# Reordering the first group of four batches: routers, one block sum and the first loads

## The chip, the cores and the metric

The kernel runs on one core of one Trainium2 chip. The metric is the device time of one execution in microseconds (us). Five engines work side by side, each on its own queue of instructions: PE (matrix products, its weight loads shown as PEld), DVE (vector), ACT (scalar), POOL (general) and SP, which here only issues loads and stores. The order of instructions on each engine is written out by hand in the program; semaphores make an engine wait for the data or the buffer that another one gives it.

## The reference

Four layers follow each other, each added to its input. x has 8 batches of 256 tokens with 1024 features, all in float32. Layer 0, where the change lies, is cut here to its core:

```
base   = x @ W.T
logits = x @ Wr.T + 5 * one_hot(language)          # 8 experts
gates  = softmax over the best 2 logits, 0 elsewhere
h      = x @ A[e].T for all 8 experts              # rank 16 each: 128 rows
x      = x + base + 2 * sum_e (h[e] * gates[e]) @ B[e].T
...
x = x + x @ (W1 + coeff * (2*mask - 1)) + b1       # layer 1, a mask for each batch
x = x + x @ W2[adapter].T                          # layer 2, a matrix for each batch
x = x + 2 * (x @ B3[adapter].T) @ A3[adapter].T    # layer 3, rank 16
```

The products are split: every float32 matrix is taken as a rounded part (hi) and a rest (lo), and hi x hi, lo x hi and hi x lo are summed.

## The kernel before

The batches are worked in two groups (g = 0, 1) of four, each group as two pairs of batches; `pair_of(g, 0)` is the first pair worked (p0, pair 1 in group 0) and `pair_of(g, 1)` the second (p1, pair 0). Features lie in 8 slices k of 128.

Layer 0 takes its 2x2 block product of W and the two pairs in Winograd's form: seven block products instead of eight, with sums S1 to S4 of the blocks A11 to A22 of W and sums T1 to T4 of the blocks B11 to B22 of x. `L0_PRODUCTS` lists them; each fills two slots s (halves h), and two more slots (4 and 5) hold only products of x with the experts' matrix A. So group 0 has slots 0 to 15: 0, 1 A11 x B11; 2, 3 A12 x B21; 4, 5 the second pair's expert products; 6, 7 S1 x T1; 8, 9 S4 x B22; 10, 11 S2 x T2; 12, 13 S3 x T3; 14, 15 A22 x T4. Blocks that go into a slot are numbered in order (`items`); block i is split on ACT into `whi` (hi, `highs`) and on DVE into `wlo` (lo, `lows`), with five and four buffers; so a split of hi stands five blocks ahead of the buffer's last use, a split of lo four.

`l0_slot(n)` writes one slot: first what leaves the accumulators (`l0_evacuate`: the copies U1 at slot 2 and C11 at slot 6 on ACT; V at 8, W at 10 and so on as sums on DVE), then the splits, then the slot's further works (`l0_works`, a table by slot made with `at(s, ...)`; negative keys are run ahead of the splits), then the matmuls (`l0_main`, with works in the middle of a product from the table `l0_mids`). The accumulators are tiles of a pool with two buffers; `chain` takes a new two at slots 0, 6 and 10, so slot 6 takes over the two of slots 0 to 5. `head` is slots 0 and 1 written by hand in quarters of a block, so that the first matmuls start on small loads.

The works of group 0 that matter here:

- `logits(p)`: 16 records of small matmuls into a bank, copied to `lg` by ACT. `by_token(p)` turns it over on PE (`pt`). `router(p)` is some 21 small DVE instructions, with one ACT instruction (`ex`, the exponential) two thirds of the way, and ends in the gates; `expand(p)` repeats them to 128 columns (`gx`). `gates_by_rank(p)` turns those over on PE (`pg`) and copies to `gt`. `gate(p)` multiplies `gt` with the experts' products `ph` on DVE and splits the result into `ghi` (ACT) and `glo` (DVE), which the last matmuls of slot 5 (p0) and those of slot 9 (p1) use with `lb`, the experts' B.
- `la_parts`: splits A into `laghi`, `laglo`.
- `less` (T1, T3): negates a block of x in place on ACT, and adds another block by a load that accumulates, issued by POOL. `s1_add`, `s3_add`: POOL adds the identity to a block, then such a load. `s4_add`: a copy on ACT and such a load; before the change group 0 instead adds two blocks on DVE for S4.
- `constants`: 8 small DVE instructions on the language, coefficient and adapter numbers.

SP issues the first loads one after the other in the order at the end of the kernel; each waits for the load issued eight before it.

Of the kernel before, what the change touches and what calls it, by code (L numbers as in the profile page):

```python
# [34 lines left out]
def kernel(ctx: ExitStack, tc: tile.TileContext, x, lang, coeff, ids,  # L35
# [73 lines left out]
    lbs = [cst.tile([P, K * P], FR, name=f"lb{n}") for n in range(2)]  # L109

    def load_constants():
        nc.sync.dma_start(wrs, wr)
        nc.sync.dma_start(lang_i, lang.rearrange("(a b) -> a b", a=1).to_broadcast([P, NB]))
        nc.sync.dma_start(c_sb, coeff.rearrange("(a b) -> a b", a=1).to_broadcast([P, NB]))
        nc.sync.dma_start(ids_raw, ids.rearrange("(a b) -> a b", a=1))
        nc.sync.dma_start(b1_sb, b1)
# [59 lines left out]
    def pair_of(g, j):  # L176
        return 2 * g + 1 - j
# [124 lines left out]
    def logits(p):  # L302


        g, j = p // 2, 1 - p % 2
        pl = bank(j, f"pl{p}")
        for k in range(K):
            c = 32 * (k % 4)
            mm(pl[c:c + 32, :], wrs[:, k, :], X[g][:, j, k, :], start=(k < 4), stop=(k >= 4))  # L309
        lgs[p] = gp.tile([P, N], F32, tag="lg", name=f"lg{p}", bufs=3)  # L310
        copy(lgs[p], pl)

    def by_token(p):
        pts[p] = bank(1 - p % 2, f"pt{p}")
# [80 lines left out]

    def gate(p):
        tt(gts[p], phs.pop(p), gts[p], ALU.mult)
        split_gates(p, gts[p])

    def gate_difference(g):  # L400

# [259 lines left out]
    def l0_works(g):  # L661


        p0, p1 = pair_of(g, 0), pair_of(g, 1)
        w = {}

        def at(s, *fs):
            w.setdefault(s, []).extend(fs)

        def add(name, h, src):  # L670
            nc.gpsimd.dma_start(quad(g, name)[h], src, accum_op=ALU.add)

        def s1_add(h):
            fold_quad(quad(g, "S1")[h], h)
            add("S1", h, w0[1, 2 + h])

        def s3_add(h):
            t = quad(g, "S3")[h]
            copy(flat(t), flat(quad(g, "S2")[h]))
            fold_quad(t, h)  # L680
            add("S3", h, w0[1, 2 + h])

        def s4_add(h):
            copy(flat(quad(g, "S4")[h]), flat(quad(g, "S2")[h]))
            add("S4", h, w0[0, 2 + h])

        def less(h, name, j, i):

            t = flat(quad(g, name)[h])
            nc.scalar.mul(t, t, -1.0)  # L690
            add(name, h, x[pair_of(g, j)][:, 4 * i + 2 * h:4 * i + 2 * h + 2])

        def both(f, *args):
            return [lambda h=h: f(h, *args) for h in range(2)]

        def subs(o, a, b):
            return [lambda h=h: sub(g, o, a, b, h) for h in range(2)]

        def lb_parts():
            copy(lbs[0], lb_raw)  # L700
            tt(lbs[1], lb_raw, f32(lbs[0]), ALU.subtract)

        if g == 0:
            at(1, *both(less, "T1", 1, 0), constants)
            at(2, *both(s1_add))
            at(3, lambda: router([p0]), lambda: expand(p0))
            at(4, lb_parts)
            at(-5, lambda: gate(p0))
            at(5, *subs("S2", "A11", "S1"))
            at(6, lambda: [tt(flat(quad(0, "S4")[h]), flat(quad(0, "S4")[h]),  # L710
                              flat(quad(0, "S2")[h]), ALU.add) for h in range(2)])
            at(6, lambda: router([p1]), lambda: expand(p1))
        else:
            at(0, *both(s1_add), *both(less, "T1", 1, 0))
            at(2, lambda: expand(p0))
            at(3, *subs("S2", "A11", "S1"))
            at(4, *both(s4_add))
            at(-5, lambda: gate(p0))
            at(5, lambda: expand(p1))
        at(4, *both(less, "T3", 1, 1))  # L720
        at(7, *subs("T2", "T1", "B22"))
        at(7, *both(s3_add))
        at(8, lambda: gate(p1), lambda: gate_difference(g))
        for h in range(2):
# [24 lines left out]
    def l0_mids(g):  # L749


        p0, p1 = pair_of(g, 0), pair_of(g, 1)
        if g == 0:
            return {2: lambda: by_token(p0), 3: lambda: logits(p1),
                    4: lambda: [by_token(p1), gates_by_rank(p0)],
                    7: lambda: gates_by_rank(p1)}
        mids = {0: lambda: proj_pair(1, 0), 1: lambda: rank_pair(1, 1, (0, 1)),
                2: lambda: gates_by_rank(p0), 6: lambda: gates_by_rank(p1)}
        mids.update({s: lambda: fill(2) for s in (3, 4, 5)})
        mids[-5] = lambda: fill(2)  # L760
        return mids
# [28 lines left out]
    def l0_slot(n):  # L790
        _, g, s, _ = slots[n]
        f = first[n]
        store()
        if s >= 7:
            load_unit(64 * g + s - 7)
        w = works[g]
        if s == 0 and g:
            G[g] = region(GC[g], f"c{g}", [P, 4, 4, N], F32)
        evacuate()
        l0_evacuate(g, s)  # L800
        if (g, s) == (0, 0):
# [11 lines left out]
        if g == 0 and s == 1:  # L813
            la_parts(0, 4, 8)
        if g or s > 1:
            l0_main(g, s)
        for u in merges.get(n + 1, []):
            merge_scale(u)

    def head():  # L820

        chain(0, 0)
        for s in range(2):
            for k in range(2):
                c = slice(k * 512, (k + 1) * 512)
                for i in (2 * s, 2 * s + 1):
# [6 lines left out]
                la_parts(0, 2 * s + k, 2 * s + k + 1)  # L833
                product(s, 0, [k], start=(s == 0))
                experts(0, pair_of(0, 0), 2 * s, 2 * s + k, k)
            folded.update((2 * s, 2 * s + 1))
        logits(pair_of(0, 0))


    pos_tile = {}  # L840
# [1 line left out]
    def main(n):  # L842
# [15 lines left out]
        if kind == "L1":  # L858
            if u == 0:
                hls["L2", q] = hl_tile(GX[q // 2], f"hl2_{q}")  # L860
        else:
            if u == 0:
                i = 2 - 2 * (q % 2)
                xt2 = G[q // 2][:, i:i + 2].rearrange(
                    "p j a (b t) -> p j (a b) t", b=2)
                xts[q, 2] = xt2
                xts[2 * q], xts[2 * q + 1] = xt2[:, 0], xt2[:, 1]
            if q % 2:
                if u == 1:
                    mid = [lambda: proj_pair(q - 1, 2)]  # L870
                if u == 3:
                    mid = [lambda: rank_pair(q - 1, 3, (2, 3))]
                if 5 <= u < 9:
                    mid = [lambda: fill(2)]
            if q == 1:
                if u == 13:
                    mid = [lambda: [logits(p) for p in (2, 3)]]
# [122 lines left out]
    for h in range(2):  # L1000
        for k in range(2):
            m = 2 * h + k
            load_x(0, 0, m, m + 1)
            nc.sync.dma_start(W0[0, "A11", h][:, k], w0[0, h][:, k])
            if m != 1:
                k0, k1 = ((0, 2), None, (2, 4), (4, 8))[m]
                nc.sync.dma_start(LA[0][:, k0:k1], la[:, k0:k1])
    load_x(0, 0, 4, 6)
    load_w0(0, "A12", 0)
    load_constants()  # L1010
    load_x(0, 0, 6, 8)
    load_w0(0, "A12", 1)
    for h in range(2):
        load_w0(0, "A21", h)
    load_x(0, 1, 0, 4)
# [95 lines left out]
```

## Time and profile before

| what | us or share |
|---|---|
| median of 3 runs (lowest to highest) | 623.31 (623.06 to 623.85) |
| profiled execution | 622.18 |
| its span, first to last instruction | 620.2 |
| PE busy | 598.4 (96%) |
| DVE busy | 477.2 (77%) |
| ACT busy | 383.6 (62%) |
| POOL busy | 129.8 (21%) |
| mean granted PE clock | 0.989 |
| PE busy in the first 81.34 us of the span | 67.17 |

The last row is group 0 up to slot 9. A sum of durations from the profile is compared with the profiled execution's own time, 622.18 us, of which 620.2 is the span; the median of the runs is 1.13 us above it. In the listings below a group or timeline line gives engine, line of the program, instruction, the tile written and the tiles read.

### The profile page before, as it was taken

Reading aid. Unit: us, or ns where it says so; the run is one execution under the profiler, and the core shown is the slowest. Engines: PE = TensorE matmul, PEld = TensorE weight load, DVE = VectorE, ACT = ScalarE, POOL = GpSimd, SP = SyncE. Lnnn points to the kernel's source line nnn. Section 1 sums busy time; section 2 is a strip of 40 time slices with the busy share of each in tenths; the row PEclk is TensorE's granted clock in tenths of the full one; section 3 lists DMA queues with packets and bytes.
Section 4 is the critical chain, followed back from the end, with each engine's and each line's share of the span. In section 5 each row is a group of like instructions: output and inputs, shape, how many; then the busy total and the mean of one; then the engine's idle time right before and its main releaser. Section 6 shows DMA issues by size and latency. Waiting matters only on the chain.

```text
span 620.2 us, 8932 instructions
## 1 busy us (share of the span) xinstructions
PE 598.4 (96%) x3244; PEld 502.0 (81%) x3244; DVE 477.2 (77%) x557; ACT 383.6 (62%) x453; POOL 129.8 (21%) x172
## 2 busy tenths in 40 slices
PE   8699699999999999999999999999999999999995
PEld 7477488888888888888778778888888888888884
DVE  5348967889879999777664786788987999967852
ACT  4527456668667898653545655656866798864331
POOL 0211314001321212221310132611431111321000
PEclk9899899999999999999999999999999999999998
DMA  8964379447586677589952498945758667756504
GB/s 271 379 139 69 75 182 238 148 168 278 202 272 236 226 282 273 170 337 316 293 134 41 117 239 189 257 153 185 288 171 283 224 243 266 274 166 218 191 1 135
DMA packets 39101, 129.17 MB, mean 208 GB/s; under 512 B 4754, under 2 KB 6162, under 8 KB 38290
## 3 DMA queue, kind: packets, MB, share of 16 engines
q1 hardware_dynamic: 34594, 112.62, 51.5%
q0 software_dynamic: 4320, 15.73, 13.9%
q8 instruction: 25, 0.41, 0.3%
q10 hardware_dynamic: 144, 0.26, 0.1%
q14 instruction: 18, 0.15, 0.1%
HBM read 120.21 MB, written 8.39 MB: 207 GB/s over the span
## 4 chain that ended last, share of the span: by engine, by line
PE 89%; DVE 5%; ACT 3%; issue 2%; DMA 1%; ACTq 0%; DVEq 0%
PE po L523 38%; PE mm L591 25%; PE po L532 20%; DVE wlo L68 2%; PE pl L309 1%; PE pf L462 1%; PE pb L434 1%; DVE x L68 1%; ACT whi L289 1%; ACT x L690 1%; DVE A L68 1%; PE ph L617 1%; DVE c L68 1%; PE ph L619 1%; PE ph L618 1%
## 5 line engine op out<-in xcount | busy, mean ns | idle before, releaser
L523 PE MATMUL po<-hl,whi 128*128 128x512 f32 x1016 | 254.5, 392 | 0.0
L523 PEld LDWEIGHTS po<-hl,whi 128*128 128x128 f32 x1016 | 182.8, 189 | 32.7
L68 DVE TENSOR_TENSOR wlo<-raw,whi 128x1024 fp32r<-128x1024 f32 x128 | 160.9, 1267 | 1.3 <-issue 1.2
L532 PEld LDWEIGHTS po<-hl,wlo 128*128 128x128 f32 x1016 | 137.6, 190 | 11.3 <-issue 2.5
L289 ACT CAST whi<-raw 128x1024 fp32r<-128x1024 f32 x128 | 133.7, 1048 | 17.9 <-PE mm L591 8.4
L532 PE MATMUL po<-hl,wlo 128*128 128x256 f32 x1016 | 142.3, 283 | 0.0
L591 PE MATMUL mm<-whi,whi 128*128 128x512 f32 x224 | 89.4, 399 | 4.1 <-DVE c L68 3.3
L591 PE MATMUL mm<-wlo,whi 128*128 128x512 f32 x224 | 88.6, 395 | 0.0
L236 POOL TENSOR_TENSOR raw<-raw,ident 128x128 f32<-128x128 f32 x72 | 57.5, 801 | 117.6 <-DMA raw<-in_w 100.0
L258 ACT ACTIVATE raw<-raw,negc,c 128x1024 f32<-128x1024 int32 x64 | 79.5, 1242 | 3.4 <-DMA raw<-in_mask 3.4
L591 PE MATMUL mm<-whi,wlo 128*128 128x512 f32 x224 | 71.3, 394 | 0.0
L68 DVE TENSOR_TENSOR raw<-raw,w 128x1024 f32<-128x1024 f32 x56 | 70.2, 1254 | 0.7 <-POOL w L236 0.7
L68 DVE TENSOR_TENSOR wlo<-x,whi 128x1024 fp32r<-128x1024 f32 (+1 forms) x38 | 45.0, 1193 | 32.0 <-ACT whi L289 10.5
L236 POOL TENSOR_TENSOR w<-w,ident 128x128 f32<-128x128 f32 x28 | 27.6, 985 | 168.5 <-DMA w<-in_w 122.4
L591 PEld LDWEIGHTS mm<-whi,whi 128*128 128x128 f32 x224 | 42.7, 191 | 15.5 <-issue 4.9
L591 PEld LDWEIGHTS mm<-whi,wlo 128*128 128x128 f32 x224 | 42.5, 190 | 9.7 <-DVE wlo L68 0.4
L591 PEld LDWEIGHTS mm<-wlo,whi 128*128 128x128 f32 x224 | 42.8, 191 | 8.9
L564 ACT COPY c<-po 128x512 f32<-128x512 f32 (+1 forms) x34 | 18.8, 552 | 47.0 <-PE po L532 47.0
L289 ACT CAST whi<-A 128x1024 fp32r<-128x1024 f32 x26 | 27.3, 1048 | 33.1 <-PE mm L591 15.5
L289 ACT CAST whi<-x 128x1024 fp32r<-128x1024 f32 x34 | 35.3, 1049 | 14.7 <-PE mm L591 14.7
L567 ACT ACTIVATE sum<-po,b_sb 128x512 f32<-128x512 f32 (+1 forms) x36 | 23.1, 641 | 30.7 <-PE po L532 30.7
L68 DVE TENSOR_TENSOR c<-mm,c 128x1024 f32<-128x1024 f32 x20 | 24.2, 1219 | 19.9 <-PE mm L591 19.9
(126 smaller groups left out, 534.4 us busy)
## 6 DMA issues: line engine op xcount, KB each, us to landing
raw<-in_mask SPq DMA_DIRECT2D x64, 512.0 KB, 5.0
raw<-in_w SPq DMA_DIRECT2D x64, 512.0 KB, 4.8
w<-in_w SPq DMA_DIRECT2D x28, 512.0 KB, 3.7
out<-c SPq DMA_DIRECT2D x31, 256.0 KB, 3.2
A<-in_w SPq DMA_DIRECT2D x14, 512.0 KB, 8.5
x<-in_x SPq DMA_DIRECT2D x6, 1024.0 KB, 8.4
x<-in_x POOLq DMA_DIRECT2D x12, 512.0 KB, 7.8
A<-in_w POOLq DMA_DIRECT2D x10, 512.0 KB, 7.3
```

The lines of the kernel that those rows point to most:

```text
L68: nc.vector.tensor_tensor(o, a, b, op)
L236: (eng or nc.gpsimd).tensor_tensor(t, t, ident, ALU.add)
L258: nc.scalar.activation(f32(raws[n]), raws[n], AF.Identity, bias=negc[:, b:b + 1], scale=c2[:, b:b + 1])
L289: copy(prep_hi(i), flat(source(i)))
L309: mm(pl[c:c + 32, :], wrs[:, k, :], X[g][:, j, k, :], start=(k < 4), stop=(k >= 4))
L434: mm(pb[c:c + 32, j * T:(j + 1) * T], l3b[b][:, k, :], xts[b][:, k, :], start=(k < 4), stop=(k >= 4))
L462: mm(po[:, i * T:(i + 1) * T], at[:, (m + i) * P:(m + i + 1) * P], rt, start=True, stop=True)
L523: mm(po, hi[:, c], xhl[:, k, j].rearrange("p h t -> p (h t)"), start=(k == 0), stop=False)
L532: mm(po[:, :T], lo[:, c], xhl[:, k, j, 0, :], start=False, stop=(k == K - 1))
L564: copy(xs, po[:, :, T:])
L567: nc.scalar.activation(xs, po[:, :, T:], AF.Identity, bias=b1c)
L591: mm(*args, skip_group_check=True, **kw)
```

## The change

Six things are moved or replaced, all in group 0 unless said:

1. The logits of the first pair are taken inside the head, ahead of slot 1's last quarter; the split of block 4 is written before their copy, block 5's split and the second half of A follow right after the head, before constants and block 6. Their turning over (`by_token`) ends the head instead of standing in slot 2.
2. The first pair's router is in slot 2 instead of 3, its turning over by rank in the middle of slot 3 instead of 4; `by_token` of the second pair ends slot 3 instead of standing in slot 4; the second router is in slot 5 instead of 6, its turning over in slot 6 instead of 7.
3. Constants and the S1 loads come first (slot 1), the negations and loads of T1 after them (slot 2). `lb` is split in slot 3 instead of 4, the S2 differences are made in slot 3 instead of 5.
4. S4 is made in slot 4 by two ACT copies and two accumulating loads instead of two DVE sums in slot 6.
5. The multiplication with the gates (`gate`) is separated from the split (`split_gates`); for the first pair of both groups it moves to slot 4, the split stays at slot 5.
6. The first loads: `wrs` after all of the first pair's x; A's second half later and x's last two slices earlier, both halves of A12 ahead of the constants.

`logits` now returns its copy as a function, `leave`, so that it can be written later; for the second group both pairs' matmuls are then followed by both copies.

```
@@ -109,7 +109,6 @@
     lbs = [cst.tile([P, K * P], FR, name=f"lb{n}") for n in range(2)]
 
     def load_constants():
-        nc.sync.dma_start(wrs, wr)
         nc.sync.dma_start(lang_i, lang.rearrange("(a b) -> a b", a=1).to_broadcast([P, NB]))
         nc.sync.dma_start(c_sb, coeff.rearrange("(a b) -> a b", a=1).to_broadcast([P, NB]))
         nc.sync.dma_start(ids_raw, ids.rearrange("(a b) -> a b", a=1))
@@ -307,8 +306,11 @@
         for k in range(K):
             c = 32 * (k % 4)
             mm(pl[c:c + 32, :], wrs[:, k, :], X[g][:, j, k, :], start=(k < 4), stop=(k >= 4))
-        lgs[p] = gp.tile([P, N], F32, tag="lg", name=f"lg{p}", bufs=3)
-        copy(lgs[p], pl)
+
+        def leave():
+            lgs[p] = gp.tile([P, N], F32, tag="lg", name=f"lg{p}", bufs=3)
+            copy(lgs[p], pl)
+        return leave
 
     def by_token(p):
         pts[p] = bank(1 - p % 2, f"pt{p}")
@@ -395,7 +397,6 @@
 
     def gate(p):
         tt(gts[p], phs.pop(p), gts[p], ALU.mult)
-        split_gates(p, gts[p])
 
     def gate_difference(g):
 
@@ -701,26 +702,22 @@
             tt(lbs[1], lb_raw, f32(lbs[0]), ALU.subtract)
 
         if g == 0:
-            at(1, *both(less, "T1", 1, 0), constants)
-            at(2, *both(s1_add))
-            at(3, lambda: router([p0]), lambda: expand(p0))
-            at(4, lb_parts)
-            at(-5, lambda: gate(p0))
-            at(5, *subs("S2", "A11", "S1"))
-            at(6, lambda: [tt(flat(quad(0, "S4")[h]), flat(quad(0, "S4")[h]),
-                              flat(quad(0, "S2")[h]), ALU.add) for h in range(2)])
-            at(6, lambda: router([p1]), lambda: expand(p1))
+            at(1, constants, *both(s1_add))
+            at(2, *both(less, "T1", 1, 0), lambda: router([p0]), lambda: expand(p0))
+            at(3, lb_parts, *subs("S2", "A11", "S1"))
+            at(4, *both(s4_add), lambda: gate(p0))
+            at(5, lambda: router([p1]), lambda: expand(p1))
         else:
             at(0, *both(s1_add), *both(less, "T1", 1, 0))
             at(2, lambda: expand(p0))
             at(3, *subs("S2", "A11", "S1"))
-            at(4, *both(s4_add))
-            at(-5, lambda: gate(p0))
+            at(4, *both(s4_add), lambda: gate(p0))
             at(5, lambda: expand(p1))
+        at(-5, lambda: split_gates(p0, gts[p0]))
         at(4, *both(less, "T3", 1, 1))
         at(7, *subs("T2", "T1", "B22"))
         at(7, *both(s3_add))
-        at(8, lambda: gate(p1), lambda: gate_difference(g))
+        at(8, lambda: gate(p1), lambda: split_gates(p1, gts[p1]), lambda: gate_difference(g))
         for h in range(2):
             at(9 + h, lambda h=h: add("T4", h, x[p0][:, 4 + 2 * h:6 + 2 * h]))
         for i in range(4):
@@ -751,9 +748,8 @@
 
         p0, p1 = pair_of(g, 0), pair_of(g, 1)
         if g == 0:
-            return {2: lambda: by_token(p0), 3: lambda: logits(p1),
-                    4: lambda: [by_token(p1), gates_by_rank(p0)],
-                    7: lambda: gates_by_rank(p1)}
+            return {3: lambda: [gates_by_rank(p0), logits(p1)()], -3: lambda: by_token(p1),
+                    6: lambda: gates_by_rank(p1)}
         mids = {0: lambda: proj_pair(1, 0), 1: lambda: rank_pair(1, 1, (0, 1)),
                 2: lambda: gates_by_rank(p0), 6: lambda: gates_by_rank(p1)}
         mids.update({s: lambda: fill(2) for s in (3, 4, 5)})
@@ -802,6 +798,9 @@
             head()
         for work in w.get(-s, []) if s else []:
             work()
+        if (g, s) == (0, 1):
+            highs(5)
+            la_parts(0, 4, 8)
         highs(f + HI_AHEAD)
         fold(f + HI_AHEAD + 1)
         fold(f + HI_AHEAD + 2)
@@ -810,8 +809,6 @@
             work()
         for u in merges.get(n, []):
             merge_add(u)
-        if g == 0 and s == 1:
-            la_parts(0, 4, 8)
         if g or s > 1:
             l0_main(g, s)
         for u in merges.get(n + 1, []):
@@ -831,10 +828,14 @@
                     tt(prep_lo(i)[:, c], flat(source(i))[:, c], f32(his[i])[:, c],
                        ALU.subtract)
                 la_parts(0, 2 * s + k, 2 * s + k + 1)
+                if (s, k) == (1, 1):
+                    leave = logits(1)
+                    highs(4)
+                    leave()
                 product(s, 0, [k], start=(s == 0))
-                experts(0, pair_of(0, 0), 2 * s, 2 * s + k, k)
+                experts(0, 1, 2 * s, 2 * s + k, k)
             folded.update((2 * s, 2 * s + 1))
-        logits(pair_of(0, 0))
+        by_token(1)
 
 
     pos_tile = {}
@@ -874,7 +875,7 @@
                     mid = [lambda: fill(2)]
             if q == 1:
                 if u == 13:
-                    mid = [lambda: [logits(p) for p in (2, 3)]]
+                    mid = [lambda: [leave() for leave in [logits(p) for p in (2, 3)]]]
                 if u == 14:
                     mid = [lambda: [by_token(p) for p in (2, 3)]]
             if q == 3:
@@ -1002,14 +1003,16 @@
             m = 2 * h + k
             load_x(0, 0, m, m + 1)
             nc.sync.dma_start(W0[0, "A11", h][:, k], w0[0, h][:, k])
-            if m != 1:
-                k0, k1 = ((0, 2), None, (2, 4), (4, 8))[m]
+            if m % 2 == 0:
+                k0, k1 = m, m + 2
                 nc.sync.dma_start(LA[0][:, k0:k1], la[:, k0:k1])
     load_x(0, 0, 4, 6)
+    load_x(0, 0, 6, 8)
+    nc.sync.dma_start(wrs, wr)
     load_w0(0, "A12", 0)
+    nc.sync.dma_start(LA[0][:, 4:8], la[:, 4:8])
+    load_w0(0, "A12", 1)
     load_constants()
-    load_x(0, 0, 6, 8)
-    load_w0(0, "A12", 1)
     for h in range(2):
         load_w0(0, "A21", h)
     load_x(0, 1, 0, 4)
```

More of the change, by code (lines that the diff above doesn't have):

```diff
@@ L111, in load_constants @@
     def load_constants():
-        nc.sync.dma_start(wrs, wr)
         nc.sync.dma_start(lang_i, lang.rearrange("(a b) -> a b", a=1).to_broadcast([P, NB]))
@@ L309, in logits, with leave @@
             mm(pl[c:c + 32, :], wrs[:, k, :], X[g][:, j, k, :], start=(k < 4), stop=(k >= 4))
-        lgs[p] = gp.tile([P, N], F32, tag="lg", name=f"lg{p}", bufs=3)
-        copy(lgs[p], pl)
+        def leave():
+            lgs[p] = gp.tile([P, N], F32, tag="lg", name=f"lg{p}", bufs=3)
+            copy(lgs[p], pl)
+        return leave
     def by_token(p):
@@ L397, in gate @@
         tt(gts[p], phs.pop(p), gts[p], ALU.mult)
-        split_gates(p, gts[p])
     def gate_difference(g):
@@ L703, in l0_works @@
         if g == 0:
[L704 to L712, printed above, removed]
+            at(1, constants, *both(s1_add))
+            at(2, *both(less, "T1", 1, 0), lambda: router([p0]), lambda: expand(p0))
+            at(3, lb_parts, *subs("S2", "A11", "S1"))
+            at(4, *both(s4_add), lambda: gate(p0))
+            at(5, lambda: router([p1]), lambda: expand(p1))
         else:
@@ L716, in l0_works @@
             at(3, *subs("S2", "A11", "S1"))
-            at(4, *both(s4_add))
-            at(-5, lambda: gate(p0))
+            at(4, *both(s4_add), lambda: gate(p0))
             at(5, lambda: expand(p1))
+        at(-5, lambda: split_gates(p0, gts[p0]))
         at(4, *both(less, "T3", 1, 1))
@@ L722, in l0_works @@
         at(7, *both(s3_add))
-        at(8, lambda: gate(p1), lambda: gate_difference(g))
+        at(8, lambda: gate(p1), lambda: split_gates(p1, gts[p1]), lambda: gate_difference(g))
         for h in range(2):
@@ L753, in l0_mids @@
         if g == 0:
-            return {2: lambda: by_token(p0), 3: lambda: logits(p1),
-                    4: lambda: [by_token(p1), gates_by_rank(p0)],
-                    7: lambda: gates_by_rank(p1)}
+            return {3: lambda: [gates_by_rank(p0), logits(p1)()], -3: lambda: by_token(p1),
+                    6: lambda: gates_by_rank(p1)}
         mids = {0: lambda: proj_pair(1, 0), 1: lambda: rank_pair(1, 1, (0, 1)),
@@ L804, in l0_slot @@
             work()
+        if (g, s) == (0, 1):
+            highs(5)
+            la_parts(0, 4, 8)
         highs(f + HI_AHEAD)
@@ L812, in l0_slot @@
             merge_add(u)
-        if g == 0 and s == 1:
-            la_parts(0, 4, 8)
         if g or s > 1:
@@ L833, in head @@
                 la_parts(0, 2 * s + k, 2 * s + k + 1)
+                if (s, k) == (1, 1):
+                    leave = logits(1)
+                    highs(4)
+                    leave()
                 product(s, 0, [k], start=(s == 0))
-                experts(0, pair_of(0, 0), 2 * s, 2 * s + k, k)
+                experts(0, 1, 2 * s, 2 * s + k, k)
             folded.update((2 * s, 2 * s + 1))
-        logits(pair_of(0, 0))
+        by_token(1)
     pos_tile = {}
@@ L876, in main @@
                 if u == 13:
-                    mid = [lambda: [logits(p) for p in (2, 3)]]
+                    mid = [lambda: [leave() for leave in [logits(p) for p in (2, 3)]]]
                 if u == 14:
@@ L1004 @@
             nc.sync.dma_start(W0[0, "A11", h][:, k], w0[0, h][:, k])
-            if m != 1:
-                k0, k1 = ((0, 2), None, (2, 4), (4, 8))[m]
+            if m % 2 == 0:
+                k0, k1 = m, m + 2
                 nc.sync.dma_start(LA[0][:, k0:k1], la[:, k0:k1])
     load_x(0, 0, 4, 6)
+    load_x(0, 0, 6, 8)
+    nc.sync.dma_start(wrs, wr)
     load_w0(0, "A12", 0)
+    nc.sync.dma_start(LA[0][:, 4:8], la[:, 4:8])
+    load_w0(0, "A12", 1)
     load_constants()
-    load_x(0, 0, 6, 8)
-    load_w0(0, "A12", 1)
     for h in range(2):
```

## The prediction

> **What bounds the kernel now.** I read the totals, the PE's list of waits, then the timeline of PE, ACT, DVE and POOL over the first 90 us, then small windows for the clock. By the page, PE is busy 598.4 us of a 620.2 us span, so only its idle stretches can be won. The list of waits says where they are:
>
> ```profile
> engine line waited for: us in total, times, longest us
> PE ph L617 <- ACT laghi L643: 6.0, 1, 6.0
> PE mm L591 <- DVE c L68: 3.3, 2, 2.9
> PE pg L383 <- DVE gx L372: 2.8, 1, 2.8
> ```
>
> All three long ones lie in group 0 of layer 0, which is what the diff reorders. The timeline, engine by engine (start, length, engine, line; in brackets the idle time before it and its releaser):
>
> ```profile
> 20.50 1.92 PE L309 MATMUL pl<-x,wrs 128*32 128x512 f32 x16
> 28.37 0.79 PE L617 MATMUL ph<-whi,laghi 128*128 128x512 f32 x1 [5.95 <-ACT laghi L643]
> 33.39 0.40 PE L591 MATMUL mm<-whi,whi 128*128 128x512 f32 x1
> 54.24 0.49 PE L591 MATMUL mm<-glo,lb 128*128 128x512 f32 x1 [0.23 <-DVE glo L68]
> 68.05 0.66 PE L383 MATMUL pg<-ident,gx 128*128 128x128 f32 x4 [2.83 <-DVE gx L372]
> 74.35 0.76 PE L591 MATMUL mm<-whi,whi 128*128 128x512 f32 x1 [2.90 <-DVE c L68]
> 81.34 0.39 PE L591 MATMUL mm<-ghi,lb 128*128 128x512 f32 x1
> ...
> 22.49 0.59 ACT L311 COPY lg<-pl 128x512 f32<-128x512 f32 x1 [8.82 <-PE pl L309]
> 25.81 2.00 ACT L690 ACTIVATE x<-x 128x1024 f32<-128x1024 f32 x2
> 27.71 0.60 ACT L643 CAST laghi<-c 128x512 fp32r<-128x512 f32 x1
> 43.16 0.21 ACT L355 ACTIVATE ex<-d 128x4 f32<-128x4 f32 x1 [3.42 <-DVE d L68]
> ...
> 40.07 0.29 DVE L327 TENSOR_REDUCE lv<-pt 128x32 f32<-128x128 f32 x1
> 44.47 0.43 DVE L372 COPY gx<-oh 128x512 f32<-128x512 f32 x1
> 70.18 2.88 DVE L68 TENSOR_TENSOR x<-x 128x1024 f32<-128x1024 f32 x2
> ```
>
> Read ACT first: it idles 8.82 us until the logits end on PE, because the copy of them stands ahead of the splits; only then come three splits, two negations and the cast of A that PE waits for. PE pays 5.95 us. And it restarts at half clock, as the windows show (after DVE, ACT and POOL: granted clock, DMA share, GB/s):
>
> ```profile
> 26.00:26.50 0.50, 0.00 (x0) 0.00 (x0) 0.49 (x2) 0.50 (x1) 0.00 (x0) 0.67 0.95 385
> 32.50:33.00 0.50, 0.50 (x3) 0.40 (x2) 0.00 (x0) 0.00 (x0) 0.50 (x2) 0.50 1.02 205
> 33.00:33.50 0.50, 0.50 (x4) 0.41 (x3) 0.00 (x0) 0.00 (x0) 0.08 (x1) 1.00 1.10 221
> 74.00:74.50 0.50, 0.15 (x1) 0.18 (x2) 0.50 (x2) 0.00 (x0) 0.11 (x1) 0.50 0.77 90
> ```
>
> What can be won between 17.01 us (end of the third quarter of the head) and 81.34 us (first matmul of slot 9): 5.95 idle; 12 matmuls from 28.37 to 33.39 in 5.02 us instead of 2.72 (2.30); 0.76 around the two gate matmuls at 53.25; 2.98 before the gate transposes; 3.06 before slot 8; 7 matmuls to 77.43 in 3.08 instead of 1.59 (1.49). Sum 16.54. The other 64.33 - 16.54 = 47.79 us are work at 0.227 us a matmul, which the change only permutes.
>
> **What the Trainium skill says.** "TensorE: Matmul & The Clock Gate", Part 1, gives a half clock after an idle window of about 3.4 us and full clock after a busy one, the window running free of the kernel. The trace agrees: the clock falls near 26.2 and 74.0 and rises near 33.0 and 77.3, multiples of 3.4 us apart. The same page calls ACT and DVE strictly first-in first-out; the 8.82 us show it. "DMA: Bandwidth & Descriptors", Issuing engines are not separate DMA queues, says transfers of SP and POOL share the engines: at 27 to 30 us 410 GB/s move, and 213 once POOL's accumulating transfers are there.
>
> **Part by part, on the new order of each engine.** I walk the queues with durations of the trace, starts about 0.07 us after the releaser, and ACT/DVE pitches of 0.95/1.14 us for 128x1024.
>
> *Loads.* The wait of each SP issue for the one eight earlier stays. In the old run a transfer landed about 1.7 us after its last byte at some 410 KB/us. Third quarter's inputs keep their places. x 6:8 then lands about 14.2 and wrs about 14.6 (before 18.3 and 15.3), A12 about 15.9 and 17.8, A's second half about 16.5, A21 about 19.5 and 20.5, the second pair's x about 25 and 27.
>
> *Logits in the head.* 16 matmuls, 1.95 us, move from 20.4 to 17.0; their inputs landed over 2 us earlier. The last quarter follows and hides the rest: ACT splits x (4) at 13.7, copies logits at 19.1, splits A12 (5) 19.6 to 20.6, casts A to 21.1, splits 6 to 22.1, copies U1 to 23.95, splits 7 to 24.95. DVE: lo of A to 21.9, lo 4 to 23.0, lo 5 to 24.1. PE ends the quarter at 22.35, transposes logits to 22.8, and waits about 0.1 for lo 4. So 5.95 and 2.30 go. Slot 2 ends at 29.65.
>
> *Router of the first pair.* DVE: 1.3 us of constants, lo 6 and 7 to 27.7, router 4.83 us by the rows above (40.07 to 44.90): gx at 32.5. ACT splits 8 (needs the second pair's x), negates T1 to about 28, and does ex at 30.7. PE wants gx in the middle of slot 3, 33.7: hidden with 1.2 us to spare. Then gate transposes, 1.95 us of logits, slot 3 ends 38.8, transposes to 39.2.
>
> *Slots 4 and 5.* 24 matmuls to 44.65. DVE has gx, lo 8, lo 9, lb, the S2 differences to 38.2, then lo 10 and 11 (their buffers come free at 38.8): in time. S4's sum leaves DVE (2.35 us) and becomes two ACT copies and two more accumulating loads; these have until 58 us, so DMA hides them. But ACT's queue from 38.8 is now split 11, split 12, two S4 copies, two T3 negations, and behind them ghi: 6.3 us, ghi at 45.2, glo on DVE at 45.9. PE wants them at 44.65: 1.1 us of waits in the place of 0.76. Gate matmuls end near 48.6.
>
> *The new stall.* On DVE behind glo stand lo 12, lo 13 (to 48.2) and then the second router, whose d is ready after 3.09 us, 51.2. Its ex now stands on ACT ahead of the C11 copies; before, the router came after them. The C11 copies empty the accumulators that slot 6 takes over, so PE waits: ex to 51.4, first copy to 52.35, PE at 52.45: 3.85 us idle. It replaces the 2.98 at the gate transposes (gx at 53.0, wanted 55.2: hidden).
>
> *Slot 8.* After slot 6, DVE needs 0.07 + 2 x 1.15 (lo 16, 17) + 2.35 to 2.88 (T2) + 1.2 (first V) = 5.9 to 6.45, PE's slot 7 lasts 5.44: 0.5 to 1.0, I take 0.8 instead of 3.06. No router stands there.
>
> *Cold clock.* Old facts: a window 79% idle (2.7 of 3.41 us, to 74.0) lowered the clock, one 61% idle (from 65.07 to 67.15) didn't. A 3.85 us stall at a random phase passes such a threshold in 55 to 90% of phases; a drop costs one window at half speed, 1.0 to 1.7. I take 1.5.
>
> *The rest.* Earlier constants, the wider S1 lead and group 1's earlier gate multiply: nothing, since from 81.34 to 300 us PE is busy without a gap in the windows and all later issues hang on its slots.
>
> Sum: new extras 0.1 + 1.1 + 3.85 + 0.8 + 1.5 = 7.35 against 16.54: 9.2 us less. The profiled execution took 622.18 (span 620.2), so one like it would take 613.0; the runs' median is 623.31, hence 614.1.
>
> **Rivals.**
> 1. *The stall at slot 6 stays warm.* Phase decides, and a little faster router would help. Without the 1.5: 612.6.
> 2. *Transfers come late.* S1's accumulating loads now start about 21 us, while x of the second pair, lb and A22 still flow; in 30.5 to 32.5 us of the old trace POOL's queue took 83% of the engines and SP's 27%. If lb lands after about 36.3 or T1 after 39.8 (I expect 33 and 37; T1 took 8.4 us from issue), lo 10 or split 12 is late and everything to ex with it, us for us. With 3 us: 617.
> 3. *C11's copies aren't held by ex*, should PE not need them: the 3.85 and 1.5 go: 608.8. Against it: the pool has two buffers and slot 0's are the two.
> 4. *Slower than before*, by rival 2's mechanism in one place: S1's loads starve the second pair's x, split 8 blocks ACT, and ex, T1 and all after it slip. It decides from a landing at about 29 us, at one us each; more than 9.2 lost needs 38.3, giving 624 at 39. Against it: before, that x landed by 28.5 and SP kept full rate until 30.
>
> **Chances.** Forecast 0.50, rival 1 0.20, rival 2 0.20, rival 3 0.05, rival 4 0.05. The range 611.5 to 617.5 takes in the first three with the ends of the cold clock (0 to 1.7), of slot 8 and of a late transfer to 3 us; outside stay rivals 3 and 4 and the later part of 2. Two runs of this kernel can be told apart by about 0.2%, 1.2 us: faster 0.94, same 0.02, slower 0.04 (rival 4 less its mild part).
>
> **What would show it.** Right: no PE wait for laghi; logits at about 17; a PE wait of 3 to 4 us before the first matmul of slot 6, released by the ACT copy of C11, after ex; slot 9 near 72 us in place of 81.34. Wrong: ACT waiting for a DMA of x, lb or T1 between 25 and 40; slot 6 starting as the gate matmuls end; or new PE waits after slot 9, which would give back what the head won.

## The result and the profile after

| | before | after |
|---|---|---|
| median, us (lowest to highest, runs) | 623.18 (622.23 to 623.85, 4) | 614.5 (613.21 to 614.83, 4) |
| profiled execution, us | 622.18 | 613.21 |
| its span, us | 620.2 | 611.0 |
| first matmul of slot 9, us from the span's start | 81.34 | 72.12 |
| from there to the end of the span, us | 538.86 | 538.88 |
| PE busy, us | 598.4 | 597.0 |

The ratio is 0.9858, with a 95% interval of 0.9839 to 0.9877. All of the difference between the two profiled executions lies ahead of slot 9: 9.22 us are gained there, and the 538.9 us behind it didn't change. The list of PE's waits in the changed kernel shows what became of the three long ones (engine, matmul, then the instruction waited for, total, number, longest):

```profile
PE mm L592 <- ACT c L734: 3.5, 1, 3.5
...
PE mm L592 <- ACT whi L288: 0.6, 1, 0.6
...
PE mm L592 <- DVE glo L68: 0.2, 1, 0.2
```

The waits for `laghi` (5.95) and for `gx` (2.83) are gone, that before slot 8 is 0.62 instead of 2.90, and one new wait of 3.53 stands before slot 6. Where each lies is in the timelines of PE and of ACT, after (start, length, engine, line; idle before and its releaser in brackets):

```profile
22.88 0.47 PE L618 MATMUL ph<-whi,laghi 128*128 128x512 f32 x1
23.35 0.50 PE L619 MATMUL ph<-wlo,laghi 128*128 128x512 f32 x1
...
45.14 0.39 PE L620 MATMUL ph<-whi,laglo 128*128 128x512 f32 x1
45.59 0.50 PE L592 MATMUL mm<-ghi,lb 128*128 128x512 f32 x1
46.32 0.50 PE L592 MATMUL mm<-glo,lb 128*128 128x512 f32 x1 [0.22 <-DVE glo L68]
...
48.77 0.39 PE L592 MATMUL mm<-ghi,lb 128*128 128x512 f32 x1
52.69 0.50 PE L592 MATMUL mm<-whi,whi 128*128 128x512 f32 x1 [3.53 <-ACT c L734]
...
66.56 0.47 PE L592 MATMUL mm<-whi,whi 128*128 128x512 f32 x1 [0.62 <-ACT whi L288]
...
72.12 0.39 PE L592 MATMUL mm<-ghi,lb 128*128 128x512 f32 x1
```

```profile
19.09 0.59 ACT L312 COPY lg<-pl 128x512 f32<-128x512 f32 x1 [3.41 <-PE pl L308]
...
39.22 2.00 ACT L288 CAST whi<-x 128x1024 fp32r<-128x1024 f32 x2 [1.93 <-PE mm L592]
41.13 1.99 ACT L685 COPY A<-A 128x1024 f32<-128x1024 f32 x2
43.03 2.00 ACT L691 ACTIVATE x<-x 128x1024 f32<-128x1024 f32 x2
44.93 0.60 ACT L394 CAST ghi<-gt 128x512 fp32r<-128x512 f32 x1
...
51.53 0.20 ACT L357 ACTIVATE ex<-d 128x4 f32<-128x4 f32 x1 [4.09 <-DVE d L68]
51.64 1.91 ACT L734 COPY c<-mm 128x1024 f32<-128x1024 f32 x2
```

Read ACT upwards from the new stall. The C11 copies begin at 51.64, though PE had finished the products that they empty at about 49.0 (last matmul at 48.77); they are next in the queue behind `ex`, and `ex` waited 4.09 us for DVE. DVE, after:

```profile
45.57 0.69 DVE L68 TENSOR_TENSOR glo<-gt,ghi 128x512 fp32r<-128x512 f32 x1 [3.43 <-ACT ghi L394]
46.18 1.22 DVE L68 TENSOR_TENSOR wlo<-x,whi 128x1024 fp32r<-128x1024 f32 x1
47.31 1.22 DVE L68 TENSOR_TENSOR wlo<-A,whi 128x1024 fp32r<-128x1024 f32 x1
48.45 0.28 DVE L329 TENSOR_REDUCE lv<-pt 128x32 f32<-128x128 f32 x1
...
51.34 0.15 DVE L68 TENSOR_TENSOR d<-mx,mx 128x4 f32<-128x4 f32 x1
```

DVE itself had been idle for 3.43 us, waiting for `ghi` on ACT, which stands behind the four S4 and T3 instructions (41.13 to 45). So one chain crosses between the two engines twice: S4 and T3 on ACT, `ghi` on ACT, `glo`, two splits and most of the router on DVE, `ex` and the copies on ACT, PE.

The wait before slot 8 is put down to a split on ACT (L288), but this can't be what ended it. ACT and DVE, after, then the same matmul in a second execution of the same program:

```profile
65.53 1.05 ACT L288 CAST whi<-A 128x1024 fp32r<-128x1024 f32 x1 [1.19 <-PE mm L592]
65.21 2.34 DVE L68 TENSOR_TENSOR c<-mm,c 128x1024 f32<-128x1024 f32 x2
...
67.54 0.47 PE L592 MATMUL mm<-whi,whi 128*128 128x512 f32 x1 [0.62 <-DVE c L68]
```

The split ends at 66.58, when the matmul of 66.56 has begun. The first of the two V sums on DVE is done near 66.4 (65.21 and half of 2.34; the semaphore of DVE for which PE waits there came at 66.43), and in the second execution, with the same wait of 0.62, V is named.

### The profile page after: what moved, and what is told of

Its sections match the earlier page's. It is cut to its first block, busy times and chain, and to the rows that moved or that the text cites. A ratio compares the mean times of both kernels' runs of the same rounds, so it can differ in the third digit from the quotient of the medians.

```text
span 611.0 us, 8941 instructions
## 1 busy us (share of the span) xinstructions
PE 597.0 (98%) x3244; PEld 500.6 (82%) x3244; DVE 474.5 (78%) x555; ACT 385.1 (63%) x455; POOL 140.3 (23%) x174
## 4 chain that ended last, share of the span: by engine, by line
PE 92%; DVE 3%; ACT 2%; issue 1%; DMA 1%; ACTq 0%
PE po L524 38%; PE mm L592 27%; PE po L533 20%; PE pl L308 1%; DVE wlo L68 1%; PE pf L463 1%; PE pb L435 1%; ACT x L691 1%; PE ph L619 1%; PE ph L618 1%; PE ph L620 1%; ACT whi L288 1%; DMA x<-in_x 1%; DVE c L68 0%; PE pb L482 0%
## 5 line engine op out<-in xcount | busy, mean ns | idle before, releaser
L288 ACT CAST whi<-raw 128x1024 fp32r<-128x1024 f32 x128 | 133.7, 1048 | 18.0 <-PE mm L592 8.4
L235 POOL TENSOR_TENSOR raw<-raw,ident 128x128 f32<-128x128 f32 x72 | 59.2, 823 | 116.9 <-DMA raw<-in_w 86.9
L235 POOL TENSOR_TENSOR w<-w,ident 128x128 f32<-128x128 f32 x28 | 34.6, 1237 | 158.3 <-DMA w<-in_w 134.1
L288 ACT CAST whi<-A 128x1024 fp32r<-128x1024 f32 x26 | 27.3, 1050 | 34.4 <-PE mm L592 16.9
L288 ACT CAST whi<-x 128x1024 fp32r<-128x1024 f32 x34 | 35.3, 1048 | 8.9 <-PE mm L592 8.9
L68 DVE TENSOR_TENSOR wlo<-A,whi 128x1024 fp32r<-128x1024 f32 (+1 forms) x30 | 35.8, 1193 | 4.7 <-ACT whi L827 2.7
```

The source lines that it names most:

```text
L68: nc.vector.tensor_tensor(o, a, b, op)
L235: (eng or nc.gpsimd).tensor_tensor(t, t, ident, ALU.add)
L288: copy(prep_hi(i), flat(source(i)))
```

## The experiments

Unless said, each is the changed kernel with one edit. Ratios are to the kernel before in the same job: its median was 623.18 for the first row, 622.05 for the four runs from the logits to the second router, 622.95 for the next four, and 622.51 for the changed kernel again and the last row. The last three columns are of the one profiled execution of each run, in us.

| run | median, us (lowest to highest, runs) | ratio [95% interval] | slot 6 at | wait there | slot 9 at |
|---|---|---|---|---|---|
| changed kernel, first runs | 614.5 (613.21 to 614.83, 4) | 0.9858 [0.9839, 0.9877] | 52.69 | 3.53 | 72.12 |
| changed kernel again | 614.5 (612.82 to 618.43, 6) | 0.9873 [0.9834, 0.9912] | 52.69 | 3.54 | 73.08 |
| logits behind the head | 619.0 (617.56 to 620.18, 6) | 0.9941 [0.9917, 0.9964] | 59.89 | 3.54 | 79.07 |
| kernel before, new loads | 621.49 (620.15 to 624.43, 14) | 0.9999 [0.9984, 1.0015] | 56.82 | none | 79.80 |
| old loads | 614.91 (611.37 to 616.39, 6) | 0.9872 [0.9841, 0.9903] | 53.31 | 3.54 | 73.62 |
| second router in slot 6 | 611.82 (611.12 to 612.95, 6) | 0.9836 [0.9812, 0.9859] | 49.01 | none | 70.66 |
| T3 later | 611.94 (609.81 to 612.79, 6) | 0.9820 [0.9795, 0.9846] | 50.78 | 2.47 | 68.62 |
| S4 on DVE | 610.19 (609.21 to 612.51, 6) | 0.9804 [0.9778, 0.9830] | 50.64 | 2.46 | 68.29 |
| router begun early | 607.93 (607.01 to 610.27, 6) | 0.9767 [0.9740, 0.9793] | 48.26 | none | 65.99 |
| the same, T2 earlier | 608.37 (607.34 to 609.27, 5) | 0.9765 [0.9740, 0.9791] | 49.02 | none | 66.08 |
| the same, lo 4 in the head | 607.86 (606.68 to 608.47, 6) | 0.9752 [0.9720, 0.9783] | 49.87 | none | 66.92 |

**Theory and rivals.** The theory of the prediction: the gain comes from the logits' place in the head (the order on ACT), and what limits it is the stall before slot 6, made by the place of `ex` ahead of the C11 copies. A rival: the new order of loads is what removes the waits. Another: the stall comes from something else, so moving the router doesn't remove it.

### Logits behind the head again

```diff
-                if (s, k) == (1, 1):
-                    leave = logits(1)
-                    highs(4)
-                    leave()
                 product(s, 0, [k], start=(s == 0))
...
             folded.update((2 * s, 2 * s + 1))
+        leave = logits(1)
+        highs(4)
+        leave()
         by_token(1)
```

> The changed kernel, but the first pair's logits stand on PE behind the last quarter of the head again, as before the change (split of block 4 still ahead of their copy on ACT). Main theory (ACT's queue behind the logits made the 5.95 us wait): the copy leaves ACT near 23.0, block 5 and the cast of A near 24.5, lo of block 4 near 26.4, so slot 2 begins about 3 us later than in the changed kernel, at 26 instead of 23.3; 617.5 us, up to 1.7 more if the clock falls. Rival (the order of the loads brought the gain): no change against the changed kernel, 614.5.

The timeline of PE for this run:

```profile
24.41 0.66 PE L319 MATMUL pt<-ident,lg 128*128 128x128 f32 x4 [0.71 <-ACT lg L312]
25.88 0.50 PE L618 MATMUL ph<-whi,laghi 128*128 128x512 f32 x1 [0.80 <-ACT laghi L644]
27.74 0.79 PE L619 MATMUL ph<-wlo,laghi 128*128 128x512 f32 x1 [1.36 <-DVE wlo L68]
```

The waits sum to 2.87 us, and PE restarts at half clock: the 14 matmuls from 27.74 to 33.86 take 6.12 us instead of 14 x 0.227 = 3.18, so 2.94 more. By medians the edit costs 4.5 us. Of the 6.95 us by which this execution's slot 9 is later, 5.8 are these two terms; the rest is a slow start of PE in the head, for which see the last section. All loads were in their new order, and waits are back, so the rival that the loads remove them fails here.

But only 2.87 of the 5.95 us came back. ACT shows where the rest stays away:

```profile
23.77 0.58 ACT L312 COPY lg<-pl 128x512 f32<-128x512 f32 x1 [8.44 <-PE pl L308]
...
25.20 0.62 ACT L644 CAST laghi<-c 128x512 fp32r<-128x512 f32 x1
```

ACT still waits for the logits, 8.44 us, but the cast of A begins 1.43 us after their copy. In the kernel before it began 5.22 us after it (22.49 to 27.71), behind three splits and two negations. So about half of the wait went with the place of the logits; the other half I put down to the order of ACT's work behind them, which was not run by itself. All that this run leaves in place of the change is worth the other 3.1 us to the kernel before (622.05 to 619.0).

### The loads alone, and the old loads in the changed kernel

The kernel before, with part 6 of the change:

```diff
     def load_constants():
-        nc.sync.dma_start(wrs, wr)
...
     load_x(0, 0, 4, 6)
-    load_w0(0, "A12", 0)
-    load_constants()
     load_x(0, 0, 6, 8)
+    nc.sync.dma_start(wrs, wr)
+    load_w0(0, "A12", 0)
+    nc.sync.dma_start(LA[0][:, 4:8], la[:, 4:8])
     load_w0(0, "A12", 1)
+    load_constants()
```

> The kernel before, with only the new order of the first loads. Main theory: every load of group 0 had landed before its turn, so nothing moves: 623.2 plus or minus 0.6, the wait for laghi stays near 6 us. Rival (loads in order of use bring the gain): most of the 8.7 us, 615 to 618.

Nothing moved: the interval of the ratio is 0.9984 to 1.0015 (both kernels ran below the 623.2 of my expectation in this job), and PE's wait for `laghi` is the same 5.95 us:

```profile
28.04 0.80 PE L616 MATMUL ph<-whi,laghi 128*128 128x512 f32 x1 [5.95 <-ACT laghi L642]
```

That slot 9 is at 79.80 in this one execution, and not at 81.34, is the clock: it was at half speed from 67.3 to 70.7, while slot 7 ran and slot 8 had to wait for V anyway, and not behind that wait. The opposite run, the changed kernel with part 6 undone:

```diff
     def load_constants():
+        nc.sync.dma_start(wrs, wr)
...
     load_x(0, 0, 4, 6)
-    load_x(0, 0, 6, 8)
-    nc.sync.dma_start(wrs, wr)
     load_w0(0, "A12", 0)
-    nc.sync.dma_start(LA[0][:, 4:8], la[:, 4:8])
-    load_w0(0, "A12", 1)
     load_constants()
+    load_x(0, 0, 6, 8)
+    load_w0(0, "A12", 1)
```

> The changed kernel with the old order of the first loads. Main theory: the logits in the head want x 6:8 at about 17.5, which landed at 18.3 before; PE waits 0.7 to 1.4 us there, and nothing else: 615.2 to 616.0. Rival (loads in order of use bring the gain): back to 620 or more.

Here my expectation missed the cause. The logits began at 17.12 and lasted 1.93 us without a wait: the last two slices of x landed at 17.33, not at 18.3, and the matmuls on them are also issued last. What came instead was a wait of 0.63 us at slot 2, for lo 4. The order of loads is worth less than these runs can tell, 614.91 against 614.5; a difference of some 2 us either way would hide in the two intervals. As an account of the gain the rival is out: the loads alone bring nothing, and without them the wait for `laghi` doesn't come back. The wait for lo 4 on PE, and what DVE and POOL did then in this run:

```profile
24.02 0.50 PE L620 MATMUL ph<-wlo,laghi 128*128 128x512 f32 x1 [0.63 <-DVE wlo L68]
...
21.81 2.16 DVE L68 TENSOR_TENSOR wlo<-x,whi 128x1024 fp32r<-128x1024 f32 x1
...
22.01 2.25 POOL L236 TENSOR_TENSOR A<-A,ident 128x128 f32<-128x128 f32 x2
```

and the run with the logits behind the head shows both without an overlap, DVE's split later than POOL's sums:

```profile
22.35 1.17 POOL L235 TENSOR_TENSOR A<-A,ident 128x128 f32<-128x128 f32 x2
...
26.46 1.22 DVE L68 TENSOR_TENSOR wlo<-x,whi 128x1024 fp32r<-128x1024 f32 x1
```

The split grew from 1.22 to 2.16 us and POOL's two sums of S1 from 1.17 to 2.25. The Trainium skill, "SBUF — State Buffer", Who interferes with whom, says that a DVE instruction with two operands in SBUF contends with a GpSimd instruction that reads SBUF; both are of that kind, and the two traces agree.

### The second router in slot 6, after the C11 copies

```diff
-            at(5, lambda: router([p1]), lambda: expand(p1))
+            at(6, lambda: router([p1]), lambda: expand(p1))
...
-                    6: lambda: gates_by_rank(p1)}
+                    7: lambda: gates_by_rank(p1)}
```

> The changed kernel with the second router back in slot 6 behind the C11 copies, and its turning over in slot 7. Main theory (ex ahead of C11 on ACT makes the wait before slot 6): that wait of 3.5 us goes and the cold clock behind it; DVE is then late with the second router, and a wait of about 2.7 us comes before slot 8 (V behind the router and T2): 611 to 612.5 us. Rival (something else holds slot 6, or the router belongs in slot 5): the wait before slot 6 stays, or the time rises above 614.5.

ACT and PE of this run:

```profile
47.81 1.02 ACT L734 COPY c<-mm 128x1024 f32<-128x1024 f32 x1 [0.34 <-PE mm L592]
49.21 1.02 ACT L734 COPY c<-mm 128x1024 f32<-128x1024 f32 x1 [0.38 <-PE mm L592]
...
55.43 0.20 ACT L357 ACTIVATE ex<-d 128x4 f32<-128x4 f32 x1 [3.31 <-DVE d L68]
```

```profile
63.51 0.70 PE L592 MATMUL mm<-whi,whi 128*128 128x512 f32 x1 [2.90 <-DVE c L68]
```

With `ex` behind them, the copies now wait for PE, not PE for them, and slot 6 has no wait. That shows the cause of the stall. But the router's DVE work now stands ahead of V, and 2.90 us come back before slot 8, with half clock behind them: from there to slot 9 it takes 7.15 us, in the changed kernel 5.56. By medians against the kernel before of each job 10.2 us are gained; the changed kernel gains 8.0 and 8.7 in its two jobs. The intervals of the ratios overlap, so that this order is the better one isn't shown.

### What makes `ex` late: T3 and S4 on ACT

The prediction derived the stall from `ghi` being late behind ACT's S4 copies and T3 negations. Each pair is moved away by itself. T3's to slot 6:

```diff
-        at(4, *both(less, "T3", 1, 1))
+        at(6 if g == 0 else 4, *both(less, "T3", 1, 1))
```

> The changed kernel with one move: the two T3 negations of group 0 (1.9 us of ACT, and their loads) go from slot 4 to slot 6, so they no longer stand ahead of ghi on ACT. Main theory (ACT's queue ahead of ghi sets ghi, glo, the second router, ex and C11 one for one): ghi 1.9 us earlier, no wait at the gate matmuls, slot 6 begins about 1.65 us earlier, at 51.0 instead of 52.7, with a wait of 3.0 to 3.1 us; 612.8 us, or 611.5 if the clock stays up. Rival (the second router is set by its own data on DVE): slot 6 begins within 0.4 us of 52.7, 614.5.

S4 back to two sums on DVE (part 4 of the change undone):

```diff
-            at(4, *both(s4_add), lambda: gate(p0))
+            at(4, lambda: gate(p0))
+            at(6, lambda: [tt(flat(quad(0, "S4")[h]), flat(quad(0, "S4")[h]),
+                              flat(quad(0, "S2")[h]), ALU.add) for h in range(2)])
```

> The changed kernel with S4 of group 0 made by the two DVE sums in slot 6 again, as before the change, in place of two ACT copies and two accumulating loads. Main theory: ACT's queue ahead of ghi is 1.9 us shorter, as with T3 later, slot 6 begins near 51.0; the sums fall into the idle time that DVE has in slot 6 (55.8 to 60.2) and cost nothing: 612.8. Rival (S4 off DVE is what made room): the sums delay T2 and V, slot 8 begins later, 615 to 617.

ACT with T3 later:

```profile
41.12 1.99 ACT L685 COPY A<-A 128x1024 f32<-128x1024 f32 x2
43.02 0.61 ACT L394 CAST ghi<-gt 128x512 fp32r<-128x512 f32 x1
...
49.62 0.21 ACT L357 ACTIVATE ex<-d 128x4 f32<-128x4 f32 x1 [4.09 <-DVE d L68]
```

`ghi` moves from 44.93 to 43.02 and `ex` from 51.53 to 49.62, both by the 1.91 us of the two instructions removed. Slot 6 begins 1.91 us earlier, but its wait falls by 1.06 only (3.53 to 2.47, where I expected 3.0 to 3.1): the other 0.85 is mostly the wait around the gate matmuls (0.72), which also went. S4 on DVE does the same on ACT (`ghi` at 42.89, slot 6 at 50.64). In both profiled executions the gain at slot 9 is larger, 3.5 and 3.83 us. From slot 6 to slot 9 they take 17.84 and 17.65 us where the changed kernel takes 19.43: in both the windows show the clock at 1.00 from 49 to 57 us, so a stall of 2.5 us left it up in these two executions. With S4 on DVE the median is 2.6 us under the 612.8 that I expected, for which I had not counted on the clock. Part 4 of the change, taken by itself, thus costs time: 610.19 without it, 614.5 with it, and the intervals of the ratios don't meet.

### The second router begun early

With T3 later as above, the second router is split at `ex`: its first part is written in slot 4, its end behind `glo`, ahead of the slot's other splits.

```diff
...
-            at(5, lambda: router([p1]), lambda: expand(p1))
+            ends = []
+            at(4, lambda: ends.append(router_start([p1])))
+            at(-5, lambda: split_gates(p0, gts[p0]), lambda: ends.pop()(), lambda: expand(p1))
...
```

> The changed kernel with T3 later, and the second router cut in two: its part up to d in slot 4 behind the first gate multiply, where DVE idles 3.4 us for ghi, and ex and the rest behind glo, ahead of slot 5's splits. Main theory: the wait before slot 6 goes (C11's copy is done near 48.4, slot 6 begins near 48.5 instead of 52.7), the clock stays up, 0.7 us stay before slot 8: slot 9 near 66.4 instead of 72.1, 608.8 us. Rival (PE is then held by other work of DVE or ACT): no better than 612.

DVE and ACT of this run:

```profile
41.89 0.28 DVE L329 TENSOR_REDUCE lv<-pt 128x32 f32<-128x128 f32 x1
...
44.78 0.16 DVE L68 TENSOR_TENSOR d<-mx,mx 128x4 f32<-128x4 f32 x1
44.85 0.68 DVE L68 TENSOR_TENSOR glo<-gt,ghi 128x512 fp32r<-128x512 f32 x1
```

```profile
45.03 0.20 ACT L363 ACTIVATE ex<-d 128x4 f32<-128x4 f32 x1 [1.55 <-DVE d L68]
...
47.06 1.02 ACT L742 COPY c<-mm 128x1024 f32<-128x1024 f32 x1
```

The router's 3 us fill the gap in which DVE otherwise waits for `ghi`; `ex` runs at 45.03, 6.5 us earlier, and the copies at 47.06 no longer hold PE. Slot 6 begins without a wait, the wait before slot 8 is 0.39, slot 9 begins at 65.99. This version beats both kernels: 607.93, ratio 0.9767 [0.9740, 0.9793]. In the same job T3 later alone has 611.94, so beginning the router early is worth about 4 us of it. S4 is still on ACT here; the two were not tried together.

### Two refinements

T2's differences in slot 6 instead of 7, on top of it:

```diff
-        at(7, *subs("T2", "T1", "B22"))
+        at(6 if g == 0 else 7, *subs("T2", "T1", "B22"))
```

> As the run with the router cut in two, and T2's two differences from slot 7 to slot 6, into DVE's idle time, so that V is no longer behind them. Main theory: the last 0.7 us before slot 8 go too: 608.1 us. Rival: V isn't held by T2, no difference to the run without it.

The wait before slot 8 went, but in this execution lo 4 was 0.70 us late at slot 2, again beside POOL's sums (2.22 us for the split), and the time is the same, 608.37. To take that away, A's casts and lo 4 are written in the head, ahead of the copy of the logits:

```diff
                     highs(4)
+                    la_parts(0, 4, 8)
+                    lows(4)
                     leave()
...
             highs(5)
-            la_parts(0, 4, 8)
```

> On top of the split second router and the later T2 differences: the casts of A's slices 4 to 7 and block 4's lo are written before slot 1's last quarter leaves, ahead of the copy of the logits, so that they don't run beside POOL's identity sums. If the overlap of DVE and POOL is what made lo 4 late at slot 2 (0.70 us there), lo 4 takes 1.2 us, PE doesn't wait at slot 2, and the time is 607.3 to 608, slot 9 near 65.4. If the wait only moves (to the copy of the logits, or to block 5's lo), no gain: 608.4 as without it.

DVE of this run:

```profile
17.32 1.22 DVE L68 TENSOR_TENSOR wlo<-x,whi 128x1024 fp32r<-128x1024 f32 x1
22.38 1.26 DVE L68 TENSOR_TENSOR wlo<-A,whi 128x1024 fp32r<-128x1024 f32 x1 [3.83 <-ACT whi L288]
```

The mechanism is as expected: 1.22 us, finished before POOL's sums begin at 20.16, and no wait at slot 2. Slot 9 is nevertheless at 66.92 in the profiled execution, not at 65.4, because its head began with some 10 matmuls at half speed (about 2 us). The median, 607.86, can't be told from 607.93 or 608.37. So whether this is worth its half microsecond stays open.

### The changed kernel once more

> The changed kernel once more, unchanged, on the chip of the next run. 613 to 616 us, with the waits of the first trace at slot 6 (3.4 to 3.6 us behind the C11 copies) and slot 8 (about 0.6), since both follow from the order of ACT and DVE alone. What may differ is the clock: if the half-speed windows run free of the kernel, the head's first matmuls or the restart at slot 6 may be at half speed here and not there, worth 1 to 2 us either way. If the stall itself set the clock, it would fall at the same place again.

The windows of the first execution (after the length PE, PEld, DVE, ACT, POOL busy; then granted clock, DMA share, GB/s):

```profile
51.00:51.50 0.50, 0.00 (x0) 0.00 (x0) 0.45 (x3) 0.00 (x0) 0.00 (x0) 1.00 1.08 213
...
53.50:54.00 0.50, 0.50 (x3) 0.44 (x2) 0.50 (x1) 0.50 (x2) 0.00 (x0) 0.70 1.02 197
...
57.00:57.50 0.50, 0.50 (x6) 0.37 (x4) 0.00 (x0) 0.00 (x0) 0.00 (x0) 0.89 0.00 0
```

and of the second:

```profile
51.00:51.50 0.50, 0.00 (x0) 0.00 (x0) 0.45 (x3) 0.00 (x0) 0.00 (x0) 0.91 1.16 229
...
57.00:57.50 0.50, 0.50 (x2) 0.35 (x2) 0.00 (x0) 0.00 (x0) 0.00 (x0) 0.50 0.00 0
...
58.00:58.50 0.50, 0.50 (x6) 0.50 (x4) 0.00 (x0) 0.00 (x0) 0.00 (x0) 0.76 0.00 0
```

The instructions are the same, and PE restarts at 52.69 in both. In the first the clock falls at about 53.7 and is back near 57.1, one window of some 3.4 us; in the second it falls near 51.4, during the stall, and comes back only near 58.2, two windows. Slot 9 is 0.96 us later in the second. So with the same stall the clock falls at another place, and the stall alone doesn't decide whether it falls either. One run with the old loads took 611.37 us at a mean clock of 0.998, and one window at half speed would cost 0.0028 of the mean; its profiled execution has the same stall of 3.54 and two windows. Two runs with T3 later, at 612.52 and 612.79 us with mean clocks of 0.995 and 0.994, point to a fall in spite of the shorter stall: the half clock at the end of the span takes at most 0.0036 in the profiled executions.

## Why the prediction was right

The forecast was 614.1, the result 614.5; by the profiled execution 9.2 us were forecast ahead of slot 9 and 9.22 came. Extras between 17.01 and slot 9 in the profile after: 72.12 - 17.01 = 55.11, less the 47.79 of pure work, 7.32 where the prediction had 7.35. To meet it so closely is partly luck: errors of up to 0.4 us in the terms cancel, the profiled execution was the fastest of its four, and in the second execution slot 9 came 0.96 later. Its terms, each taken as the pitch between matmuls less 0.227 per matmul:

| term | predicted, us | measured, us |
|---|---|---|
| lo 4 at slot 2 | 0.1 | 0.24 |
| gate matmuls of slot 5 | 1.1 | 0.72 |
| stall before slot 6 | 3.85 | 3.69 |
| slot 8 | 0.8 | 0.78 |
| half clock | 1.5 | 1.72 |
| rest, not placed | | 0.17 |

- *Logits in the head.* Right in what it forecast: laghi's wait and the half clock after it are gone, and `lg` is copied at 19.09 (forecast 19.1). Undoing the logits' place brings 2.87 us of waits and a half clock of 2.94 us back; the other half of the wait I put down to the new order on ACT, which the walk has and which no run took by itself. The term for lo 4 was too small. I had taken the split at its 1.22 us; it took 1.48 beside POOL's sums, which the wider S1 lead had moved there.
- *First router and the gate transposes.* `ex` at 31.25 (forecast 30.7) and `gx` ready at 33.0 (32.5), with nothing waiting: hidden as said.
- *Slots 4 and 5.* `ghi` was done at 45.5 and `glo` at 46.3 (forecast 45.2 and 45.9), behind the queue of ACT that the prediction lists. Slot 5 ended at 45.37, 0.7 later than in the walk (44.65), so less of the lateness of `ghi` showed on PE, and the term was 0.38 too large; of the 0.7, 0.14 is what lo 4 took beyond the 0.1 of the walk, the rest small pitches at the turns between kinds of matmul that I had left out.
- *The new stall.* Right in its place, its releaser and its size, 3.53 us in the list of waits and 3.69 by pitch; PE restarted at 52.69 (forecast 52.45). The run with the router behind the C11 copies shows that `ex` is what holds them; the runs with T3 and S4 moved show that it is `ghi` that makes `ex` late.
- *Slot 8.* 0.62 us in the list and 0.78 by pitch, inside the 0.5 to 1.0 of the working, and ended by V on DVE, as forecast; the split on ACT that the list names ended too late to be it. The run with T2's differences earlier, which stand ahead of V, shows it: there this wait is gone.
- *Cold clock.* One window lost 1.72 us; in a second execution two windows lost about 1 us more. So the bound of 1.0 to 1.7 for a drop was too tight on its upper side: a window in which PE is idle at first need not bring the clock back. The profile before had such a case, half clock from 26.2 to 33.0. In the second execution PE was busy for about 2 of the first low window's 3.4 us (52.69 to some 54.8), and the clock stayed down for another.
- *Loads.* Hidden, as the forecast had it against rivals 2 and 4: x of the second pair landed at 24.5 and 28 (forecast 25 and 27), lb at 32 (33), the first block of T1 at 37.7 (37), and ACT waited for no load between 25 and 40. The forecast had the logits' inputs land over 2 us earlier by the new order; the logits didn't need it: undone, the order changes nothing that these runs can tell.
- *The rest at nothing.* 538.88 against 538.86 us behind slot 9.

What the working didn't say, though its numbers held it: part 4 of the change, S4 from DVE to ACT, isn't neutral. It was priced at nothing by the slack of the loads, while its two copies (1.9 us) were counted in ACT's queue ahead of `ghi`. The two belong together, and their sum is a loss of about 2 us at slot 6 and, with the clock, 3 to 4 by the ratios (0.9804 against 0.9858 and 0.9873).

## What to carry to other kernels

When a step is moved up, follow its one instruction on the other engine: the exponential of 0.2 us on ACT, not the router's 3 us on DVE, stood ahead of the copies that PE needed and held them. Work taken from a busy engine (DVE, 77%) and given to one with 37% idle time still costs if it lands ahead of a short instruction that a chain waits for; split such a chain at the crossing, and put its first part where the other engine waits anyway. Moving T3 out of that chain and starting the router in the gap gave about 6 us more (607.93 against 614.5); S4 back on DVE, by itself, gave about 4 (610.19).

## What the runs showed of the hardware

- DVE and POOL slow each other where both read two operands from SBUF: the split of 128x1024 took 1.22 us alone and 1.26 to 2.22 beside POOL's two 128x128 sums, and these took 0.87 to 1.17 without a split beside them and 2.25 to 2.64 with one.
- The granted clock comes in windows of about 3.4 us, whose phase differs from execution to execution of one kernel. Within an execution the changes lie whole windows apart, from the first rise on (5.91, 53.70 and 57.11; 7.04, 51.41 and 58.24, which is 14 and one, and 13 and two windows). The Trainium skill, "TensorE: Matmul & The Clock Gate", Part 1, says that the window runs free of the kernel; the two executions with the same restart at 52.69 agree.
- How much of a window PE is idle goes with the fall. An estimate from the starts of matmuls at 0.227 us each: the windows at whose end the clock fell were idle for 70% and 71% (the changed kernel twice) and 64% (old loads). With T3 later and with S4 on DVE an edge of the windows, at 50.05 and 49.93, cut the stall in two, and the windows were idle for 56% and 21%: no fall. The prediction's pair, 79% and 61%, fits. At another phase the same stall of 2.5 us could lie within one window, for over 70% of it.
- The first matmuls of the head, at about 6 us, ran at full speed in some executions and at half in others. With lo 4 in the head they came 0.43 us apart until 10.6 us:

```profile
6.76 0.63 PE L598 MATMUL mm<-wlo,whi 128*128 128x512 f32 x1
7.19 0.63 PE L598 MATMUL mm<-whi,wlo 128*128 128x512 f32 x1
```

The column of the granted clock reads 1.00 there, but the trace has no record of the clock so early: its first, of full clock, begins at 10.94 us. It begins at 9.92 with the logits behind the head, at 7.43 with the old loads and at 7.04 in the second execution of the changed kernel, and in each of the four the pitch falls from 0.43 to 0.23 us there. In all others it begins by 6.1 us, ahead of the first of these matmuls, and none came 0.43 apart. So this is the same clock, and the time of its first rise differs between executions of one program (5.91 and 7.04 for the changed kernel). It is worth up to 2 us in a single execution, which is more than the last two refinements could bring.
